# Local attention over eight units in one sequence, with key and query projections spread over its steps

## The chip, the cores and the metric

One core of a Trainium2 chip runs the whole program. The metric is the device time of one execution in microseconds (us), as the median of several runs. Beside it there is one profiled execution, from which all durations of single instructions come.

## The reference, cut to what matters

The input is a batch of 16 images of 64 x 64 pixels with 256 channels, in float32. Two layers follow each other, each with a group normalisation ahead of it and a residual addition behind it.

```python
# layer 0: linear attention over all pixels of an image (8 heads of 32)
x = x + _L0_conv_ref(_gn(x), L0_conv_w_qkv, L0_conv_w_out)
# layer 1: every pixel attends to the 7 x 7 pixels around it (8 heads of 32)
x = x + _L1_conv_ref(_gn(x), Wq, bq, Wk, bk, Wv, bv, emb0, emb1)

# inside layer 1
kp = _unfold(k, KSZ).reshape(B, H, W, HEADS, HS, K) + e.reshape(HEADS, HS, K)   # K = 49
scores = jnp.einsum('bhwnd,bhwndk->bhwnk', qh, kp)
attn = jax.nn.softmax(scores, axis=-1)
out = jnp.einsum('bhwndk,bhwnk->bhwnd', vp, attn)
```

The term `e` is a positional embedding: for the first four heads it depends on one axis of the 7 x 7 window, for the last four on the other.

## The kernel before, in words

**Layout.** An image lies in SBUF channel by channel: two tiles of 128 channels x 4096 pixels. Pixels are grouped into eight *strips* of 512 (`strip`, L463): a strip is a band of eight image columns over all 64 rows; strip 0 holds both edges. The order in which strips are treated is written out in `ORDER` and `KEYED` (top of the file). The instructions of TensorE, ScalarE, VectorE and SyncE stand in the order in which the program states them (`manual_schedule` with `ORDERED`); each engine works through its own list and waits on semaphores. All transfers are issued by SyncE, in that order too, at most eight of them in flight.

**One image** goes through these stages.

1. Layer 0 (`layer0`, L533 to L688): projections (L549), exponentials (L553), the context matmuls against the image's tokens (L567, the tokens come through `load_tokens`, L475), and the output products (L667), which add the residual to x.
2. Positional products and values. `positional_products` (L721) multiplies x with the positional weights; `positional` (L732) evacuates them from PSUM into the query tile `qq`, by `evacuate` (L710): ScalarE at L713, VectorE at L715. `store_rings` (L743) writes them to DRAM (`pos`); `load_rings` (L755) reads them back, shifted, into 16-partition strips of `qq` beside the query rows, together with a constant mask `io["ring"]` (L760, L761). The positional part of the scores thus becomes a part of the contraction. The values are projected strip by strip (`values_products`, L763, matmuls at L769), evacuated at L778 and written to a padded image `vpad` in DRAM (L783, L788). The PSUM for them comes from `banks()` (L392), which goes round four pairs of banks: the two tiles `double[0]` and `double[1]` of two banks each (called pd in the profile) and the four tiles `single` (ps) as two pairs.
3. For the first half of the heads (hg = 0) and then for the second (hg = 1): `keys_queries` (L792) projects all keys and then all queries of the half, two strips at a time (matmuls at L803), and evacuates them into `kaug` and `qq` (L713, L715). Then `local_attention` (L839) runs four *units*, in the order `UNITS`; a unit is a band of 16 image columns. The last pair of queries of a half is done behind the first step of its attention.

**A unit** is worked in nine *chunks* of eight key rows, two chunks to a step, the last alone: five steps. A step issues, on TensorE: the scores of its chunks (`scores`, L849, matmuls at L866, to one of the two pd tiles, then the exponential on ScalarE, L875 or L878, into a tile e), the weighted values of the step before (`weighted`, L912, L910; the sums of a unit stay in ps), and the softmax sums of the step before that (`summed`, L923, L940, into two banks). Between the two, VectorE adds the overlapping rows of neighbouring chunks (`both_chunks`, L891, L895), which the sums wait for. At a unit's end, ScalarE copies the weighted values out of PSUM (L1002), VectorE turns and inverts the sums (`finish`, L942: L947, L951, L952, L953), GpSimd multiplies (L966) and adds the residual (L974), and the finished strips are sent out (`store_out`, L1099, L1102).

**Values of a unit.** `load_window` (L827, L836) reads a unit's values from `vpad` into a window tile, four transfers for all nine chunks at once. There are two window tiles; the next unit but one is loaded when a unit has ended. The tokens of layer 0 use the same two tiles.

**The next image** is prepared meanwhile (`between0`, L1104, and `between1`, L1122): loading of its strips (L1113, L470), their statistics (L483), the group statistics with two small matmuls (`group_steps`, L268 and L277, in a part of a pd tile that `next_bank`, L403, names), the first two normalised strips (L303) and the first tokens.

At the start of each half, TensorE first fills the four pd banks with a large negative number (L983), since not every score position is written.

Of the kernel before, what the change touches and what calls it, by code (L numbers as in the profile page):

```python
# [10 lines left out]
F32 = mybir.dt.float32  # L11
# [8 lines left out]
P = 128  # L20
# [20 lines left out]
UNITS = (1, 2, 3, 0)  # L41
KEYED = (2, 3, 4, 5, 6, 7, 1, 0)
ORDER = (4, 5, 6, 7, 0, 1, 2, 3)
EDGE = (5, 3)

# [330 lines left out]
def attention_fast(tc, io, ok):  # L376
# [3 lines left out]
    with ExitStack() as ctx:  # L380
# [5 lines left out]
        turn = [0, 0]  # L386
# [5 lines left out]
        def banks():  # L392

            i = turn[1] % 4
            turn[1] += 1
            if i >= 2:
                return single[2 * i - 4 : 2 * i - 2], (0, 1)
            return [double[i][:, j] for j in range(2)], (i, i)

        def bank(name):  # L400
            return psum2()[:, 0]

        def next_bank(name):  # L403

            return double[(turn[0] + 1) % 2][:, 0, 64:]
# [43 lines left out]
        work = ctx.enter_context(tc.tile_pool(name="work", bufs=6))  # L449
        tail = ctx.enter_context(tc.tile_pool(name="tail", bufs=1))  # L450
        vwin = ctx.enter_context(tc.tile_pool(name="vwin", bufs=2))
# [4 lines left out]

        def window(name):
            return vwin.tile([P, 2 * NB * P], F32, tag="vw", name=name)
# [11 lines left out]
        def load_half(b, k):  # L470
            x = halves(b)[0][k]
            for s in ORDER:
                nc.sync.dma_start(x[:, strip(s)], xc[b, :, k, strip(s)])

        def load_tokens(b, q):  # L475

            t = window(f"xtok{b}_{q}")[:, : 8 * (C + 1)].rearrange("p (t c) -> p t c", c=C + 1)
            nc.gpsimd.memset(t[:, :, C : C + 1], 1.0)
            nc.sync.dma_start(t[:, :, :C], xt[b, q])
            return t  # L480
# [52 lines left out]
        def layer0(b, x, xn, mean, rstd, xtok, ready, midway=None):  # L533
# [30 lines left out]
            def context(p):  # L564
                for t in range(2):
                    for hg in range(2):
                        nc.tensor.matmul(  # L567
                            pc[hg][:, : C + 1],
                            eq[p][:, t, C + hg * P : C + (hg + 1) * P],
                            xtok[p // 4][:, 2 * (p % 4) + t],  # L570
                            start=(p == 0 and t == 0),
                            stop=(p == 15 and t == 1),
                        )
# [8 lines left out]
            for p in range(16 + 1):  # L582
# [6 lines left out]
                if 1 <= p <= 16:  # L589
                    context(p - 1)  # L590
                    if p % 4 == 0 and p // 4 + 1 < 4:
                        xtok[p // 4 + 1] = load_tokens(b, p // 4 + 1)
# [48 lines left out]
            w4 = window(f"w4_{b}")[:, : 8 * C].rearrange("p (h g c) -> p h g c", h=4, g=2)  # L641
# [113 lines left out]
        def load_rings(hg):  # L755
            for h in range(4):
                p0 = 64 * (h % 2) + 32
                row = pos[hg][0, RING, h]
                src = bass.AP(row.tensor, row.offset, [[4 * W, RING], [SLOTS * 4 * W, W], [1, W]])
                nc.sync.dma_start(qq[p0 + RING * hg : p0 + RING * hg + RING, h // 2], src)  # L760
                nc.sync.dma_start(qq[p0 + RING * (1 - hg) : p0 + RING * (1 - hg) + RING, h // 2], io["ring"])  # L761
# [30 lines left out]
        def keys_queries(b, hg, x):  # L792

            for what in range(2):
                for i in range(0, NS, 2):
                    if what and i == NS - 2:
                        yield
                    ps, engines = banks()
                    pair = KEYED[i : i + 2]
                    wgt = wq if what else wk  # L800
                    for a in range(2):
                        for k in range(2):
                            nc.tensor.matmul(  # L803
                                ps[a],
                                wgt[:, k, hg * P : (hg + 1) * P],
                                x[k][:, strip(pair[a])],
                                start=(k == 0),
                                stop=(k == 1),
                            )
                    for a in range(2):  # L810
                        for h in range(4):
                            rows = slice(h * HD, (h + 1) * HD)
                            d0 = 64 * (h % 2)
                            for u, p0, m, w, view in pieces(pair[a]):
                                src = view(ps[a][rows])
                                if what:
                                    dst = placed(qq[d0 : d0 + HD, h // 2], hg)[:, :, w : w + m]
                                else:
                                    dst = kaug[h // 2][d0 : d0 + HD, u, PAD : PAD + W, p0 : p0 + m]
                                dst = by_rows(dst, src)  # L820
                                if what and hg:

                                    order = "p r w -> p w r" if len(src.shape) == 3 else "p g r w -> p w g r"
                                    dst, src = dst.rearrange(order), src.rearrange(order)
                                evacuate(engines[a], dst, src, bias[rows, 2 * what + hg : 2 * what + hg + 1])

        def load_window(b, hg, t):  # L827


            vw = window(f"vw{b}_{hg}_{t}").rearrange("p (j c d) -> p j c d", j=2, d=P)  # L830
            v = vpad[b % 2]
            for j in range(2):
                for e, u in enumerate((2 * t + 2 * j, 2 * t + 1)):
                    row = v[u, 0, 0, hg * P : (hg + 1) * P]
                    src = bass.AP(row.tensor, row.offset, [[C, 64], [64 * C, NB], [1, P]])
                    nc.sync.dma_start(vw[64 * e : 64 * e + 64, j], src)  # L836
            return vw

        def local_attention(b, hg, x, y, vw, queries, after_scores, between, stored):  # L839
# [3 lines left out]
            outs, zs = single[:2], single[2:]  # L843
# [5 lines left out]
            def scores(t, c):  # L849
                ps = psum2()  # L850
                lo, hi = span(c)
                m = 16 * (hi - lo)
                for pl in range(2):
                    for e, u, w0, w1 in ((0, 2 * t, 0, 8), (1, 2 * t + 1, 2, 16), (0, 2 * t + 2, 10, 16)):
                        for ab in range(2):
                            rows = slice(64 * ab, 64 * ab + 64)
                            q = qq[rows, pl].rearrange("p (a c) -> p a c", c=W)
                            if hg == 0:
                                q = q[:, lo:hi, 16 * t + w0 : 16 * t + w1]
                                to = ps[64 * e : 64 * e + 64, ab, pl * m : (pl + 1) * m]  # L860
                                to = to.rearrange("p (r w) -> p r w", w=16)[:, :, w0:w1]
                            else:
                                q = q[:, 16 * t + w0 : 16 * t + w1, lo:hi]
# [9 lines left out]
                e = work_tile(f"e{b}_{hg}_{t}_{c}")[:, : 4 * m]  # L873
# [8 lines left out]
            def rows_of(c, e, r0, r1):  # L882
# [8 lines left out]
            def both_chunks(c, e, before):  # L891

                r0 = 8 * c - 2 * PAD
                part = rows_of(c, e, r0, 8 * c)
                nc.vector.tensor_tensor(part, part, rows_of(c - 1, before, r0, 8 * c), ALU.add)  # L895

            def products(to, j, h, c, e, r0, r1, stationary, **flags):
# [14 lines left out]
            def weighted(c, e, vw):  # L912
                if c == 0:

                    for i, to in enumerate(outs):
                        rows = slice(64 * i, 64 * i + 64)
                        nc.tensor.matmul(to, nb[rows], bits[rows, :1].to_broadcast([64, 512]), start=True, stop=False)
                for j in range(2):
                    for h in range(4):
                        v = vw[:, j, c, h * HD : (h + 1) * HD]  # L920
                        products(outs[j], j, h, c, e, *span(c), v, start=False, stop=(c == NB - 1))

            def summed(c, e):  # L923

                lo, hi = span(c)
                m = 16 * (hi - lo)
                r0, r1 = max(8 * c - 2 * PAD, 0), min(8 * c + 8 - 2 * PAD, W)
                for i in range(2):
                    a, z = max(r0, 32 * i), min(r1, 32 * i + 32)
                    for h in range(4 if a < z else 0):  # L930
                        pl, ab = divmod(h, 2)
                        pr = e[:, ab, pl * m : (pl + 1) * m]
                        dst = zs[i][h * HD : (h + 1) * HD]
                        if hg == 0:
                            pr = pr[:, 16 * (a - lo) : 16 * (z - lo)]
                            dst = dst[:, 16 * (a - 32 * i) : 16 * (z - 32 * i)]
                        else:
                            pr = pr.rearrange("p (w r) -> p w r", w=16)[:, :, a - lo : z - lo]
                            dst = dst.rearrange("p (w r) -> p w r", w=16)[:, :, a - 32 * i : z - 32 * i]
                        nc.tensor.matmul(dst, ones, pr, start=True, stop=True)  # L940

            def finish(i, t, r, pvs):  # L942

                for k in range(2):


                    nc.vector.transpose(r[:, k], zs[k])  # L947
                yield
                turned = r.rearrange("p k (a c) -> p (k a) c", c=HD)
                rc = small.tile([P, 2, 32], F32, tag="rc", name=f"rc{b}_{hg}_{t}")  # L950
# [579 lines left out]
```

## Time and profile before

| | |
|---|---|
| median of 3 runs | 5796.24 us (5793.12 to 5801.21) |
| the profiled execution | 5803.41 us, its span 5801.6 us |
| mean granted TensorE clock | 0.961 |
| TensorE matmuls busy | 5233.0 us of the span |
| VectorE, ScalarE, GpSimd busy | 3450.4, 2196.3, 1345.2 us |
| scores L866 | 27648 matmuls, 939.7 us busy |
| weighted values L910 | 18432 matmuls, 573.0 us busy |
| sums L940 | 10240 matmuls, 406.0 us busy, 150.1 us idle before them |
| key and query projections L803 | 2048 matmuls in four groups |
| overlap additions L895 | 1024, 758 ns each in the mean |
| evacuations L713 and L715 | 648 to 758 ns each for 32 x 512, in most groups |
| window loads L836 | 512 transfers of 288 KB |
| DMA | 540.81 MB, mean 93 GB/s |

How to read it: a group of instructions has the line of the kernel that issued it, its engine, its operation and its tiles; then its count, its busy time, the mean of one in ns, and the idle time of the engine just ahead of it with what ended that idle time ("releaser"). A float32 matmul of the program appears as two passes. A releaser "issue" means that the profile shows nothing that the engine waited for. The granted clock is a share of TensorE's full clock. In a table of stages the columns are: the stage in us, its length, the busy time of PE (TensorE matmuls), PEld (its weight loads), DVE (VectorE), ACT (ScalarE) and POOL (GpSimd), each with a count, then the clock, the mean busy share of the 16 DMA engines, and GB/s.

### The profile page before, as it was taken

What the parts mean: (1) busy time and instruction counts of PE and PEld (TensorE: products, weight loads), DVE (VectorE), ACT (ScalarE), POOL (GpSimd) and SP (SyncE); (2) the same over time, 40 slices, a digit from 0 to 9 for tenths busy, and PEclk for the clock granted to TensorE, in tenths of its full rate; (3) what the DMA queues carried; (4) which work ended last, traced back from release to release, by engine and by line L of the source; (5) the groups of instructions that cost most, each with busy time, mean ns of one, the idle gap of its engine ahead of it and who ended that gap; (6) DMA issues with size and microseconds to landing.
All of it is one profiled execution on the core that took longest, in us unless ns stands there. A gap on an engine that the chain in (4) does not pass through costs nothing.

```text
span 5801.6 us, 169268 instructions
## 1 busy us (share of the span) xinstructions
PE 5233.0 (90%) x75377; PEld 3593.3 (62%) x75377; DVE 3450.4 (59%) x5978; ACT 2196.3 (38%) x3089; POOL 1345.2 (23%) x1962
## 2 busy tenths in 40 slices
PE   7989899898998989989899898998989889898997
PEld 4656566565665666656666566665666566565665
DVE  4565656656566565665656556565575655756555
ACT  1341624426244261442514425153351533515335
POOL 3131131312313123130221302213032130321303
PEclk9999999999999999999999999999999999999999
DMA  4542725536164361644517345173450824517244
GB/s 122 108 104 50 138 58 112 108 58 131 50 121 99 62 132 45 126 94 78 120 41 132 97 78 119 34 136 93 78 120 32 149 80 90 116 31 142 80 78 88
DMA packets 751605, 540.81 MB, mean 93 GB/s; under 512 B 241408, under 2 KB 682368, under 8 KB 748416
## 3 DMA queue, kind: packets, MB, share of 16 engines
q1 hardware_dynamic: 750864, 529.89, 44.8%
q8 instruction: 592, 9.70, 0.7%
q14 instruction: 149, 1.22, 0.1%
HBM read 371.04 MB, written 158.73 MB: 91 GB/s over the span
## 4 chain that ended last, share of the span: by engine, by line
PE 75%; DVE 10%; issue 5%; ACT 5%; DMA 3%; SPq 1%; POOL 1%; DVEq 0%; ACTq 0%; POOLq 0%
PE pd L549 15%; PE pd L866 13%; PE ps L910 8%; PE pd L803 7%; PE ps L567 6%; PE ps L803 5%; PE ps L667 4%; PE pd L667 4%; ACT qq L713 4%; PE ps L940 4%; DVE e L895 3%; PE ps L769 3%; PE pd L769 3%; PE ps L724 2%; DVE qq L715 2%
## 5 line engine op out<-in xcount | busy, mean ns | idle before, releaser
L895 DVE TENSOR_TENSOR e<-e,e 128x384 f32<-128x384 f32 x1024 | 748.9, 758 | 765.7 <-PE ps L910 564.1
L866 PE MATMUL pd<-qq,kaug 64*64 64x112 f32 (+4 forms) x27648 | 939.7, 276 | 160.2 <-issue 65.0
L866 PEld LDWEIGHTS pd<-qq,kaug 64*64 64x64 f32 x27648 | 809.7, 138 | 322.3 <-issue 175.8
L549 PE MATMUL pd<-wqkv,img 128*128 128x512 f32 x2048 | 949.8, 609 | 3.2 <-DVE img L303 3.2
L553 ACT ACTIVATE eq<-pd 128x1024 f32<-128x1024 f32 x256 | 262.2, 1024 | 1077.8 <-PE pd L549 1077.8
L461 POOL TENSOR_TENSOR others<-others,rc 128x32 f32<-128x32 f32 x128 | 32.3, 252 | 2739.9 <-DVE rc L951 2739.7
L549 PEld LDWEIGHTS pd<-wqkv,img 128*128 128x128 f32 x2048 | 399.6, 196 | 412.6 <-issue 376.8
L556 DVE TENSOR_REDUCE qz<-eq 128x16 f32<-128x512 f32 x256 | 175.5, 686 | 768.4 <-ACT eq L553 768.4
L910 PE MATMUL ps<-e,vw 128*32 128x112 f32 (+1 forms) x18432 | 573.0, 260 | 62.7 <-issue 62.2
L878 ACT ACTIVATE e<-pd 128x896 f32<-128x896 f32 (+2 forms) x576 | 461.3, 835 | 423.1 <-PE pd L866 416.3
L875 ACT ACTIVATE e<-pd 128x896 f32<-128x896 f32 (+2 forms) x576 | 462.5, 838 | 404.0 <-PE pd L866 398.1
L713 ACT ACTIVATE qq<-ps,bias 32x512 f32<-32x512 f32 (+2 forms) x512 | 318.8, 648 | 740.7 <-DVE bias L708 665.5
L940 PE MATMUL ps<-e,ones 128*32 128x128 f32 (+2 forms) x10240 | 406.0, 266 | 150.1 <-DVE e L895 119.4
L910 PEld LDWEIGHTS ps<-e,vw 128*32 128x32 f32 x18432 | 416.7, 113 | 154.6 <-issue 118.5
L974 POOL TENSOR_TENSOR img<-img,r 128x320 f32<-128x320 f32 (+1 forms) x512 | 494.1, 995 | 0.0
L567 PE MATMUL ps<-xtok,eq 128*128 128x257 f32 x2048 | 483.4, 380 | 0.0
L567 PEld LDWEIGHTS ps<-xtok,eq 128*128 128x128 f32 x2048 | 387.3, 190 | 150.0 <-issue 107.1
L715 DVE TENSOR_SCALAR qq<-ps,bias 32x512 f32<-32x512 f32 (+2 forms) x416 | 311.8, 758 | 161.5 <-PE ps L803 155.5
L713 ACT ACTIVATE kaug<-pd,bias 32x512 f32<-32x512 f32 x256 | 173.9, 679 | 570.6 <-PE pd L803 567.7
L966 POOL TENSOR_TENSOR r<-r,r 128x512 f32<-128x512 f32 x256 | 342.2, 1358 | 139.8 <-DVE r L953 138.7
L940 PEld LDWEIGHTS ps<-e,ones 128*32 128x32 f32 x10240 | 253.5, 115 | 194.0 <-DVE e L895 157.4
L483 DVE BATCH_NORM_STATS2 st<-img 128x6 f32<-128x512 f32 x512 | 332.2, 680 | 9.1 <-DMA img<-in_xc 4.7
(142 smaller groups left out, 6613.3 us busy)
## 6 DMA issues: line engine op xcount, KB each, us to landing
vw<-vpad SPq DMA_DIRECT2D x512, 288.0 KB
img<-in_xc SPq DMA_DIRECT2D x256, 256.0 KB
xtok<-in_xt SPq DMA_DIRECT2D x64, 1024.0 KB
out<-img SPq DMA_DIRECT2D x256, 256.0 KB
vpad<-v SPq DMA_DIRECT2D x112, 512.0 KB
qq<-pos SPq DMA_DIRECT2D x128, 256.0 KB
qq<-in_ring SPq DMA_DIRECT2D x128, 256.0 KB
pos<-qq SPq DMA_DIRECT2D x128, 112.0 KB
```

What stands on the lines that cost most here:

```text
L549: nc.tensor.matmul(ps[:, t], xn[k][:, n0 : n0 + P], n.wqkv_sb[:, k, : 2 * C], start=(k == 0), stop=(k == 1))
L567: nc.tensor.matmul(pc[hg][:, : C + 1], eq[p][:, t, C + hg * P : C + (hg + 1) * P], xtok[p // 4][:, 2 * (p % 4) + t], start=(p == 0 and t = ...
L667: nc.tensor.matmul(py[a], w4[rows, h, hg, co * P : (co + 1) * P], qv[rows, 4 * hg + h, 8 * HD * i : 8 * HD * (i + 1)], start=(h == 0 and h ...
L713: nc.scalar.activation(dst, src, AF.Identity, bias=bias)
L803: nc.tensor.matmul(ps[a], wgt[:, k, hg * P : (hg + 1) * P], x[k][:, strip(pair[a])], start=(k == 0), stop=(k == 1),)
L866: nc.tensor.matmul(to, kaug[pl][rows, u, 8 * c : 8 * c + 8].rearrange("p r w -> p (r w)"), q, start=True, stop=True,)
L875: nc.scalar.activation(e.rearrange("p (a n) -> p a n", a=2), ps[:, :, : 2 * m], AF.Exp)
L878: nc.scalar.activation(e.rearrange("p (x r) -> p x r", r=hi - lo), src, AF.Exp)
L895: nc.vector.tensor_tensor(part, part, rows_of(c - 1, before, r0, 8 * c), ALU.add)
L910: nc.tensor.matmul(dst, stationary, pr, **flags)
L940: nc.tensor.matmul(dst, ones, pr, start=True, stop=True)
L974: nc.gpsimd.tensor_tensor(yv, xv, by_rows(add[:, :, a - w0 : e - w0], xv), ALU.add)
```

## The change

- The two halves' four units each become **one sequence** of eight (`SEQUENCE`), with 42 steps instead of twice 24. A blank of the pd banks is written ahead of the first two chunks of units 0 and 4.
- `keys_queries` is gone. A **job** projects the keys of one strip or the queries of half a unit (32 rows x 16 columns, `job_products`) into one bank, `single[3]`, and is evacuated in the next step (`place_job`), on ScalarE or VectorE (`job_engine`). 28 jobs stand in the steps 0 to 29 (`JOBS`); four (`AHEAD`) stand between the last value strips. A query job has six matmuls where a strip had two, since a unit is cut from three strips.
- The sums have **one bank** instead of two. They are written in three groups of rows (`SUMS`), each turned and inverted before the next is written (`reciprocals`); `LATE` says which chunks are summed in which step.
- The values are projected in the two pd tiles alone.
- Windows are loaded **by chunk pairs**: after a step's weighted values, that part of the window is filled for the unit two further on. The two window tiles are fixed tiles `vbuf`, with the chunk as the outer index; tokens are loaded in parts as well.
- The rings of the second half go to a quarter-size tile `qx` for its first unit and to quarters of `qq` for the others (`load_quarter`, in steps 19, 21 and 23).
- The work pool has 7 tiles instead of 6; the strip order is turned (6, 7, 0, 1, ...); the next image's first half of channels is loaded strip by strip from step 22, with its statistics in steps 27 to 34, group statistics in steps 35 to 37 in `single[3]`, and its first two normalised strips in steps 38 and 39. Outputs leave one strip per step (`send`).

```diff
-UNITS = (1, 2, 3, 0)
+SEQUENCE = ((0, 1), (0, 2), (0, 3), (0, 0), (1, 2), (1, 3), (1, 0), (1, 1))
 KEYED = (2, 3, 4, 5, 6, 7, 1, 0)
-ORDER = (4, 5, 6, 7, 0, 1, 2, 3)
+ORDER = (6, 7, 0, 1, 2, 3, 4, 5)
+LATE = ((0, 1), (2,), (3, 4, 5), (6, 7), (8,))
+SUMS = ((0, 18), (18, 42), (42, 64))
+AHEAD = (("k", 0, 2), ("k", 0, 3), ("k", 0, 4), ("q", 0, 1, 0))
+JOBS = {
+    0: ("q", 0, 1, 1),
+    1: ("k", 0, 5),
+    2: ("k", 0, 6),
+    3: ("q", 0, 2, 0),
+    5: ("q", 0, 2, 1),
...
+    29: ("q", 1, 1, 1),
+}
...
+        def load_rings():
+            for h in range(4):
+                dynamic_ring(0, qq, h, 0, W)
+                p0 = 64 * (h % 2) + 32 + RING
+                nc.sync.dma_start(qq[p0 : p0 + RING, h // 2], io["ring"])
+            for h in range(4):
+                dynamic_ring(1, qx, h, 32, 16)
...
+        def job_products(job, x, to):
+            what, hg = job[:2]
+            columns = slice(hg * P, (hg + 1) * P)
+            if what == "k":
+                for k in range(2):
+                    nc.tensor.matmul(to, wk[:, k, columns], x[k][:, strip(job[2])], start=(k == 0), stop=(k == 1))
+                return
...
+            def reciprocals(k, a, rc):
+                r0, r1 = SUMS[a]
+                n0, m = r0 // 2, (r1 - r0) // 2
+                to = turns[(3 * k + a) % 2][:, : HD * m]
+                nc.vector.transpose(to, sums_of(a))
+                z = to.rearrange("p (a c) -> p a c", c=HD)[:, :, 0]
+                nc.vector.reciprocal(rc[:, n0 : n0 + m], z)
+                watch(others, z, m)
...
             for step in range(len(groups) + 2):
                 new = None
+                if job:
+                    place_job(job, spare, job_engine(step - 1))
                 if step < len(groups):
                     k, g = groups[step]
                     new = (k, g, [(c, scores(k, c)) for c in range(2 * g, min(2 * g + 2, NB))])
+                    after_scores(step)
                 if held:
                     k, g, es = held
                     for c, e in es:
                         weighted(k, c, e)
+                    read(k, g)
...
                 if late:
                     k, g, es = late
                     kept += es
                     for c, e in kept:
                         if c in LATE[g]:
                             summed(k, c, e)
                     kept = [(c, e) for c, e in kept if c not in LATE[g]]
+                job = JOBS.get(step)
+                if job:
+                    job_products(job, x, spare)
                 if held:
                     for c, e in es:
                         if c:
                             both_chunks(SEQUENCE[k][0], c, e, before)
...
+        def job_engine(step):
+            return step % 5 not in (1, 4)
...
                 for i, s in enumerate(KEYED):
-                    pv = first[i] if i < 2 else banks()[0]
+                    pv = [double[i % 2][:, j] for j in range(2)]
...
+                    if i == 2:
+                        fold_bias(mean, wk, (0, 1), single[0])
+                        fold_bias(mean, wq, (2, 3), single[0])
                     if i == 3:
-                        load_rings(0)
+                        load_rings()
+                    if 3 <= i < 7:
+                        job = AHEAD[i - 3]
+                        job_products(job, x, single[i - 3])
+                        place_job(job, single[i - 3], 1)
+                    if i in (4, 5, 6, 7):
+                        load_window(b, i // 2 - 2, *((0, 4) if i % 2 == 0 else (4, NB)))
```

## The prediction

> **What bounds the kernel now.** I read, in order: busy time by engine, the stages of one image, TensorE's waits, then the PE and DMA timelines where these waits lie. The image is the one whose layer 0 starts at 2203.6 us and whose successor starts at 2561.0 us (357.4 us; all times below are us in it).
>
> ```profile
> PE 5233.0 (90%) x75377; PEld 3593.3 (62%) x75377; DVE 3450.4 (59%) x5978; ACT 2196.3 (38%) x3089; POOL 1345.2 (23%) x1962
> ```
>
> TensorE is the bound, but a tenth of the span it stands. Next, the stages (us, busy per engine, granted clock, DMA share, GB/s): value products; first-half projections; first-half attention; second-half projections; second-half attention.
>
> ```profile
> 2295.00:2363.19 68.19, 67.20 (x725) 55.26 (x721) 43.37 (x88) 7.61 (x9) 1.10 (x2) 1.00 0.30 58
> 2363.19:2390.49 27.30, 24.94 (x64) 10.75 (x61) 21.08 (x29) 17.88 (x29) 0.00 (x0) 1.00 1.03 162
> 2390.49:2460.71 70.22, 61.05 (x1778) 48.91 (x1776) 39.63 (x59) 38.71 (x56) 20.83 (x24) 0.90 0.62 134
> 2460.71:2493.98 33.27, 31.41 (x121) 14.56 (x117) 25.77 (x37) 21.15 (x34) 5.87 (x8) 0.95 0.95 117
> 2493.98:2561.02 67.04, 52.61 (x1725) 43.90 (x1724) 46.66 (x70) 34.32 (x50) 23.45 (x27) 0.96 0.42 110
> ```
>
> From 2363.19 on, TensorE idles 2.4 + 9.2 + 1.9 + 14.4 = 27.8 us, and the lowest clocks stand there. Who it waits for, over the whole run (us, times, longest):
>
> ```profile
> PE ps L940 <- DVE e L895: 119.4, 129, 3.0
> PE pd L983 <- ACT qq L713: 67.4, 32, 2.4
> PE pd L866 <- issue: 65.0, 56, 3.9
> PE ps L910 <- issue: 62.2, 50, 2.9
> PE pd L866 <- DVE gnm L270: 24.3, 15, 2.1
> ```
>
> Divided by 16 images: sums on the overlap additions 7.5; blanks on the query evacuation 4.2; "issue" 9.8 with L940's 29.6; scores on the next image's statistics 2.2 (with L279's 10.5); and the two first exponentials of each half (30.3 and 28.9) 3.7. Both starts are seen here:
>
> ```profile
> 2383.89 3.60 PE L803 MATMUL ps<-img,wqn 128*128 128x512 f32 x8
> ...
> 2390.17 0.39 PE L983 MATMUL pd<-bits,nb 32*128 32x512 bf16 x2 [2.36 <-ACT qq L713]
> 2390.49 1.36 PE L866 MATMUL pd<-qq,kaug 64*64 64x64 f32 x48
> ...
> 2401.64 2.56 PE L866 MATMUL pd<-qq,kaug 64*64 64x112 f32 x48 [1.91 <-ACT e L875]
> ...
> 2410.71 1.36 PE L866 MATMUL pd<-qq,kaug 64*64 64x64 f32 x48
> ...
> 2425.14 1.36 PE L866 MATMUL pd<-qq,kaug 64*64 64x64 f32 x48
> ```
>
> The last two are the first scores of successive units: 14.4 us, less 1.35 idle between them, is **13.0 us of TensorE work per unit** (2506.01 to 2521.80 less 2.9 gives the same). Last, the DMA under the values and projections, in stages: ring stores; value stores; ring loads; value stores; windows.
>
> ```profile
> 2344.00:2353.00 9.00, 8.77 (x41) 7.74 (x42) 7.38 (x15) 0.00 (x0) 0.00 (x0) 1.00 0.89 135
> 2353.00:2359.00 6.00, 6.00 (x29) 5.29 (x28) 2.64 (x4) 0.00 (x0) 0.00 (x0) 1.00 1.01 319
> 2359.00:2379.00 20.00, 19.74 (x82) 10.36 (x81) 13.46 (x21) 8.46 (x13) 0.00 (x0) 1.00 1.19 119
> 2379.00:2386.00 7.00, 7.00 (x17) 3.04 (x16) 5.37 (x9) 5.01 (x11) 0.00 (x0) 1.00 0.89 289
> 2386.00:2403.00 17.00, 12.73 (x176) 7.26 (x178) 7.29 (x10) 13.59 (x23) 0.00 (x0) 0.87 1.05 210
> ```
>
> DMA is full for nearly 60 us. Today the 27 us of projections hide this; it is the cover that the change takes away.
>
> **What the Trainium skill says.** "SBUF — State Buffer", section "Door 1: The DMA port swizzle": 16 partitions reach 4 of 16 ports, measured there 104 GB/s. The ring loads write 16 partitions each; the trace has 119 GB/s for them against 319 for the value stores: it agrees. The same page, "Who interferes with whom": a VectorE operation with two SBUF inputs contends with GpSimd reads. It agrees: one overlap addition takes 0.56 us alone, 1.43 (2437.0 on) while GpSimd ends a unit. "TensorE: Matmul & The Clock Gate", "What's actually happening": idle TensorE falls to half clock, and needs some 3.4 us of work to return. It agrees: after the 2.85 us wait that ends at 2558.2 the next image's first matmul shows 1222 ns where its median is 592. Its "LDWEIGHTS" section: a weight load takes columns / 1.2 ns, 107 ns for 128; no row here shows it bare.
>
> **The change, part by part.** One image, from the first ring loads on.
>
> *Start of attention.* The eight first-half ring transfers are issued where they were (after the fourth value strip), behind the same stores, so they should land when they do now, **2379**. TensorE gets there as follows. It has value strips one and two done at 2340.3; the third now reuses the first pair of banks, freed only after VectorE's positional evacuations (to 2343.9 in the new pairing: 8 x 0.92 from 2336.5) and two value evacuations (1.25): at 2345.2, a new wait of 4.9. Six strips of 3.5, bias folds of 1.8 and half clock (1.5) for the first give 2345.2 + 24.3 = 2369.5; four jobs ahead, 4 x 1.76 (16 projection passes take 7.03, a job is 4 of them), give 2376.5. So it waits 2.5 us more for the rings, and the first wait costs nothing of its own: it lies under the rings. First scores at 2379 instead of 2390.5, with 4 of 32 jobs done instead of nearly 32.
>
> *Work from there.* 8 units x 13.0 = 104.0. Key jobs 13 x 1.76 = 22.9. Query jobs 15: six short matmuls of 160, 256 and 96 columns in place of two of 512, written to PSUM in short runs. Floor 1.75 (same columns), ceiling 2.4 (every short pass held to the 196 ns that a weight load shows); the scores, also written in short runs, reach 0.9 columns per ns against 1.2 of the projections; I take 2.0, so 30.0. Blanks 4 x 0.39 = 1.6. Sums: 36 matmuls per unit, not 40, in one bank: -1.0 in all. Together 157.5, to 2536.5.
>
> *Evacuations* move into the steps. A step with a job is 3.1 scores + 1.6 weighted + 1.0 sums + 1.8 job = 7.5 on TensorE; ScalarE has 4 x 0.7 + 2 x 0.84 = 4.5, VectorE, for the ten jobs that it places, 4 x 0.75 + 2 x (0.56 to 1.43) + statistics 0.65 + a third of the reciprocals 0.6 = up to 7.1. Behind the evacuation in ScalarE's queue stand that step's exponentials, for which TensorE asks 4.7 us into the next step; behind VectorE's stand the additions, asked for one step later. Both have 3 us to spare; TensorE hides them. Without that cover each job step would grow by up to 3 us.
>
> *Waits.* The second half's start vanishes (1.9 + 1.8, and its share of half clock), as do the first half's (2.4 + 1.9), one drain (0.6) and the statistics wait, since its bank is no longer a score bank (2.4). What stays: additions and one drain 3.5 of 7.4 (GpSimd's tail now starts a step earlier, so less of it falls on the drain); "issue" 6 of 10.1, because most of these stalls lie in or just after the 1.15 MB window bursts (2418, 2432, 2451, 2513), which become five of at most 256 KB; bounds 3 and 12. New small waits 1 (scores of a unit's first chunk on queries placed a step before). Half clock 4 of 7.8. Sum 14.5 of 35.6; bounds 8.5 and 29.
>
> *Queues.* SyncE issues 20 window transfers per unit instead of 4, each waiting for the weighted matmuls of its chunk pair; output stores that wait for GpSimd (7 us) stand before them. The windows are wanted ten steps later, so nothing is late. The second half's rings follow in quarters, six steps ahead.
>
> *Sum.* 2536.5 + 14.5 = 2551.0 against 2561.0: -10. I round to **-9 us per image**, the rings being 1 us uncertain. 16 x 9 = 144: 5803.4 (span 5801.6, and 1.8 around it) - 144 = 5659 for a profiled execution; this one is 7 above the median of the runs (5796.2), so 5652, say **5650**.
>
> **The rivals.**
> *Fetch and additions are cured* (stalls 8.5): -16 per image, 5803 - 256 - 7 = 5540. For it: steps are longer by a job, and bursts small. Against: "issue" stalls are not proven to come from bursts; the initial backlog now meets dense matmuls.
> *Part of the cover is missed*: rings or query jobs cost 4 to 8 us more (query jobs at 2.4 alone are 6): 5710 to 5790.
> *Slower: the DMA backlog takes the projections' place.* The first weighted matmuls, about 2388, need the first window, queued behind rings, 0.25 MB of the second half's rings (2.2 us) and a value store (1.5); at 195 GB/s its half lands near 2386. If instead the window comes only when all of today's backlog is through (2402), TensorE stands 14 us with 28 jobs still ahead: +5 per image, 5796 + 80 = 5876. It decides from a first weighted matmul later than 2397. For it: the DMA is saturated, SyncE holds eight transfers in flight. Against: the first window is issued ahead of the last three value stores.
> That the change does not do what it says I exclude: the built order has the jobs between the steps.
>
> **How the numbers follow.** Forecast 0.55 (5600 to 5700); cured 0.13; part missed 0.12 (0.03 of it within 0.2%, what a measurement of this kernel can tell from no change); backlog 0.20 (0.02 within). Faster 0.77, same 0.05, slower 0.18. The range from 5520 to 5790 leaves out the backlog and little of the cured case.
>
> **What would show it.** No projection stage; first scores some 11 us earlier after the value products, waiting for ring transfers about 2.5 us; value products waiting 4 to 5 us for a value evacuation; no wait on L270 by scores; "issue" under 110 us in all; query jobs at 1.75 to 2.4 us. Wrong if scores wait for rings over 6 us, if weighted matmuls wait for the window, or if job steps exceed 8 us.

## The result, and the profile after

The changed kernel takes **5892.39 us** in the median (5889.42 to 5896.39, 4 runs) against 5798.73 us before (5793.12 to 5804.82, 4 runs beside them): a ratio of **1.0162**, 95% interval 1.0144 to 1.0179. It is slower by 1.6%; the forecast was 5650 us. The profiled execution's span is 5887.6 us, its clock 0.971 (before 0.961).

First the image that the prediction worked in, in two stages: values and jobs ahead, from the first value products after the bias; attention. The columns are the stretch, its length, busy time (and count) of PE, PEld, DVE, ACT and POOL, the granted clock, the DMA share and GB/s. Before:

```profile
2335.96:2390.49 54.53, 51.68 (x210) 33.57 (x208) 40.29 (x61) 24.44 (x36) 0.00 (x0) 1.00 0.88 153
2390.49:2561.02 170.53, 145.07 (x3618) 107.37 (x3616) 112.07 (x164) 94.18 (x140) 50.15 (x59) 0.93 0.61 121
```

After:

```profile
2370.88:2416.20 45.32, 36.22 (x189) 28.53 (x188) 19.14 (x31) 17.49 (x24) 0.00 (x0) 0.96 0.89 126
2416.20:2599.83 183.63, 160.33 (x3701) 123.75 (x3701) 109.28 (x185) 115.56 (x168) 54.50 (x95) 0.99 0.45 131
```

The first stage became 9.2 us shorter, where 11.5 was forecast; attention became 13.1 us longer. One image is not the mean: over the 14 inner images of each trace, by the starts of the matmuls, layer 0 and its outputs are 0.6 us longer (3.2 in this image), positional products to first scores 9.7 shorter (67.01 to 57.35), attention 15.0 longer (171.4 to 186.4), together +5.9. In the kernel after, attention so taken begins with the scores' wait for the rings; if that wait is put to the stage before it, as the prediction did, the stage is 7.0 shorter (67.0 to 60.0).

Whom TensorE waits for in the kernel after (us over the run, times, longest):

```profile
PE ps L1014 <- DVE turn L1020: 98.8, 61, 4.0
PE ps L854 <- DVE kaug L737: 79.9, 64, 1.4
PE pd L808 <- DVE v L817: 77.9, 16, 4.9
PE ps L854 <- ACT kaug L735: 35.9, 64, 1.0
PE pd L935 <- DMA qq<-in_ring: 34.7, 15, 3.1
...
PE pd L935 <- issue: 2.5, 2, 2.0
```

L854 and L836 are the products of query and key jobs, L735 and L737 the evacuations on ScalarE and VectorE. All waits of jobs for an evacuation, ten such lines, sum to **221 us, 13.8 per image**; before, there is no such wait. The stalls without a shown wait ("issue") fell from 157 us to 5, and all of TensorE's waits other than the jobs' from 554 to 373. So the change removed what it was expected to remove, 181 us, and paid more for one new wait; its matmuls are also busy 35 us longer (5268 against 5233). One job step of the kernel after shows it, first TensorE, then VectorE:

```profile
2469.18 1.98 PE L836 MATMUL ps<-img,w 128*128 128x512 f32 x4
2471.10 1.56 PE L935 MATMUL pd<-qq,kaug 64*64 64x112 f32 x48
2472.59 0.97 PE L979 MATMUL ps<-e,vbuf 128*32 128x112 f32 x32
2473.38 0.47 PE L1014 MATMUL ps<-e,ones 128*32 128x32 f32 x16
2475.15 2.09 PE L854 MATMUL ps<-img,wqn 128*128 128x160 f32 x12 [1.30 <-DVE kaug L737]
```

```profile
2470.34 1.25 DVE L1027 STREAM_TRANSPOSE r<-rc 128x1024 f32<-128x1024 f32 x1
2471.51 0.65 DVE L504 BATCH_NORM_STATS2 st<-img 128x6 f32<-128x512 f32 x1
2472.09 3.01 DVE L737 TENSOR_SCALAR kaug<-ps,bias 32x512 f32<-32x512 f32 x4
```

The key job's bank is full at 2471.2. VectorE starts to empty it at 2472.09, behind a transposition and a statistic, and needs 3.01 us for the four heads. The next job, to the same bank, could have started at 2473.85 (its wait is 1.30) and starts at 2475.15.

### The profile page after: what moved, and what is told of

It reads as the page before. It is cut to its first block, busy times and chain, and to the rows that moved or that the text cites. A ratio compares the mean times of both kernels' runs of the same rounds, so it can differ in the third digit from the quotient of the medians.

```text
span 5887.6 us, 177452 instructions
## 1 busy us (share of the span) xinstructions
PE 5268.3 (89%) x76401; PEld 3816.2 (65%) x76401; DVE 3075.9 (52%) x5818; ACT 2424.1 (41%) x3377; POOL 1418.3 (24%) x2690
## 3 DMA queue, kind: packets, MB, share of 16 engines
q14 instruction: 191, 1.56, 0.1%
## 5 line engine op out<-in xcount | busy, mean ns | idle before, releaser
L735 ACT ACTIVATE qq<-ps,bias 32x512 f32<-32x512 f32 (+1 forms) x864 | 599.9, 700 | 959.2 <-DVE bias L730 662.5
L935 PE MATMUL pd<-qq,kaug 64*64 64x112 f32 (+5 forms) x24192 | 787.0, 269 | 48.0 <-DMA qq<-in_ring 34.7
L854 PE MATMUL ps<-img,wqn 128*128 128x160 f32 (+2 forms) x3072 | 550.3, 329 | 140.7 <-DVE kaug L737 79.9
L854 PEld LDWEIGHTS ps<-img,wqn 128*128 128x128 f32 x3072 | 481.7, 194 | 230.4 <-DVE kaug L737 97.1
L735 ACT ACTIVATE kaug<-ps,bias 32x512 f32<-32x512 f32 (+1 forms) x704 | 414.0, 609 | 520.1 <-PE ps L836 514.6
L808 PE MATMUL pd<-wvn,img 128*128 128x256 f32 x2048 | 530.1, 416 | 81.9 <-DVE v L817 77.9
L836 PE MATMUL ps<-img,w 128*128 128x512 f32 x1024 | 502.8, 613 | 88.5 <-DVE kaug L737 25.6
L808 PEld LDWEIGHTS pd<-wvn,img 128*128 128x128 f32 x2048 | 423.6, 210 | 176.1 <-DVE v L817 84.3
L979 PE MATMUL ps<-e,vbuf 128*32 128x112 f32 (+1 forms) x18432 | 527.7, 252 | 0.7 <-issue 0.7
L588 PE MATMUL ps<-vbuf,eq 128*128 128x257 f32 x2048 | 483.6, 380 | 0.0
L1014 PE MATMUL ps<-e,ones 128*32 128x128 f32 (+1 forms) x9216 | 352.4, 265 | 111.4 <-DVE turn L1020 98.8
```

Source lines behind the costliest of these rows:

```text
L588: nc.tensor.matmul(pc[hg][:, : C + 1], eq[p][:, t, C + hg * P : C + (hg + 1) * P], tokens_of(p // 4)[:, 2 * (p % 4) + t], start=(p == 0 an ...
L735: nc.scalar.activation(dst, src, AF.Identity, bias=bias)
L808: nc.tensor.matmul(pi[:, t], x[k][:, n0 : n0 + P], wv[:, k], start=(k == 0 and t == 0), stop=(k == 1 and t == 1))
L836: nc.tensor.matmul(to, wk[:, k, columns], x[k][:, strip(job[2])], start=(k == 0), stop=(k == 1))
L854: nc.tensor.matmul(dst, wq[:, k, columns], src, start=(k == 0 and i == 0), stop=(k == 1 and i == len(parts) - 1),)
L935: nc.tensor.matmul(to, kaug[pl][rows, u, 8 * c : 8 * c + 8].rearrange("p r w -> p (r w)"), q, start=True, stop=True,)
```

## The experiments

**My theory after the result**: the one job bank is the bound. Products, four evacuations in a row and the next products take turns on it, 2.0 + 2.8 to 3.0 us and what stands ahead of the evacuation in its engine's queue, while the rest of a step is only 2.7 us. **Rivals**: another limit ends last anyway (additions, the sums bank), so that the wait only has a name; VectorE is overloaded; the smaller window transfers do harm or do nothing. Ratios are to the kernel before, run beside each on the same chip. It took 5784 to 5799 us there, so the medians of two rows can differ by up to 15 us for that reason alone; the ratios are free of it.

| run | what is altered, in the kernel after unless said | median us | ratio (95%) |
|---|---|---|---|
| after | | 5892.39 | 1.0162 (1.0144 to 1.0179) |
| e1_split | two heads on each engine | 5959.55 | 1.0307 (1.0289 to 1.0324) |
| e2_act | jobs on ScalarE alone | 5842.86 | 1.0101 (1.0084 to 1.0118) |
| e3_whole | whole windows | 5912.98 | 1.0221 (1.0204 to 1.0238) |
| e4_before_pairs | before, with chunk-pair windows | 5827.83 | 1.0080 (1.0063 to 1.0097) |
| e5_staged | bank emptied by one operation | 5715.71 | 0.9857 (0.9825 to 0.9889) |
| e6_norm | normalisations a step later | 5859.10 | 1.0101 (1.0069 to 1.0134) |
| e7_banks | four pairs of value banks | 5872.71 | 1.0125 (1.0092 to 1.0157) |
| e8_all | e5 to e7, earlier strip loads | 5586.57 | 0.9641 (0.9616 to 0.9666) |
| e9_all_recip | e8, reciprocals first | 5598.11 | 0.9663 (0.9640 to 0.9686) |
| e10_staged_whole | e5, whole windows | 5683.53 | 0.9818 (0.9793 to 0.9843) |
| e11_all_whole | e8, whole windows | 5592.32 | 0.9672 (0.9654 to 0.9691) |
| e12_staged_reload | e5, earlier strip loads | 5641.05 | 0.9748 (0.9731 to 0.9764) |

### Which engine empties the bank

```diff
-                    place_job(job, spare, job_engine(step - 1))
+                    place_job(job, spare, None)     # e1_split: evacuate(h % 2, ...) for head h
+                    place_job(job, spare, 1)        # e2_act
```

> Every job inside a step is evacuated by both engines, two heads each. Theory (the one job bank is the bound: its products wait 221 us in all, because four evacuations of 0.69 to 0.75 us in a row do not fit between two jobs): an evacuation takes 1.4 us instead of 2.8 to 3.0, the waits of the products (0.95 behind ScalarE, 1.3 behind VectorE) nearly vanish, under 40 us in all, and the time is 5892 - 190 = 5700 (5660 to 5740). Rival (another limit ends last in a step, such as the additions or the sums bank, and the wait only changes its name): the sums' waits grow by as much as the products' shrink, and the time stays above 5850.

> Every job is evacuated by ScalarE alone, none by VectorE; the number of evacuations on one engine in a row stays four. Theory (what counts is the length of the row of four, whichever engine does it): a row takes 2.76 instead of 3.0, so the products' waits stay, at 0.6 to 1.0 each, 150 to 220 us in all, and the time is 5860 (5830 to 5900). Rival (VectorE, with additions and reciprocals before the evacuation in its queue, is what is late): the 125 us of waits on VectorE's evacuations vanish, and the time is 5770.

**e1_split was a miss**, and the trace says why. The evacuation of one job, VectorE and then ScalarE:

```profile
2526.24 0.74 DVE L737 TENSOR_SCALAR qx<-ps,bias 32x512 f32<-32x512 f32 x1 [0.23 <-PE ps L854]
2527.73 0.74 DVE L737 TENSOR_SCALAR qx<-ps,bias 32x512 f32<-32x512 f32 x1 [0.75 <-ACT qx L735]
```

```profile
2527.02 0.68 ACT L735 ACTIVATE qx<-ps,bias 32x512 f32<-32x512 f32 x1 [1.28 <-DVE qx L737]
2528.51 0.68 ACT L735 ACTIVATE qx<-ps,bias 32x512 f32<-32x512 f32 x1 [0.81 <-DVE qx L737]
```

The two engines take turns: each copy waits for the other engine's. So the four copies last from 2526.24 to 2529.19, 2.95 us, as long as on one engine, and now every job holds up both queues: the scores wait 27 us for exponentials that stand behind it. This tested nothing of the theory's first half, but it agrees with it: the row is no shorter, and the waits did not shrink (267 us). The Trainium skill ("PSUM — Partial Sum Buffer", "PSUM bank collisions raise a hardware error") says that two engines may use different groups of 32 partitions of one bank at once, and that guarding by bank is the simple version. The heads are such groups, so by that page the turns need not be taken; that they come from a guard by whole bank fits the trace, but no run here tried the finer one.

**e2_act** came within what the theory said: the row is shorter (0.68 instead of 0.75 each, and nothing of VectorE's ahead of it), the waits fall from 221 to 156 us, but do not go. That VectorE alone was the trouble is excluded by that; its queue was a part of it, as the kernel is 0.6% faster.

### The bank is freed at once

```diff
+            if engine is None:      # to: a 512-pixel strip of SBUF that is free in this step
+                column = 2 * (what == "q") + hg
+                nc.scalar.activation(to, ps, AF.Identity, bias=bias[:, column : column + 1])
+                ps = to
...
-                evacuate(engine, dst, src, column)
+                moved(h, dst, src)  # heads 1, 3: nc.scalar.copy; heads 0, 2: nc.vector.tensor_copy
```

> A job's bank is emptied by one ScalarE operation of 128 x 512, bias added, into a strip of SBUF that is free in that step; from there ScalarE and VectorE move two heads each, with no bank between them. Theory (the time for which the one job bank is held, four evacuations in a row, sets a job step): it is held 0.6 us after the products instead of 2.8 to 3.0, the products' waits fall from 221 us to under 30, and the time is 5892 - 190 = 5700 (5650 to 5750), although ScalarE and VectorE together do more work. Rival (the additions, the sums bank or ScalarE's exponentials end last as soon as the bank does not): the sums' or the scores' waits take over and the time stays above 5840.

This is the test that e1 was meant to be. One job in e5_staged, on ScalarE and VectorE:

```profile
2462.46 0.69 ACT L872 ACTIVATE img<-ps,bias 128x512 f32<-128x512 f32 x1
2463.18 2.13 ACT L864 COPY qq<-img 32x512 f32<-32x512 f32 x2
```

```profile
2463.18 1.19 DVE L866 COPY qq<-img 32x512 f32<-32x512 f32 x2 [2.91 <-ACT img L872]
```

The bank is read for 0.69 us. From SBUF both engines move heads to the same tile at the same time, so in e1_split it was not the tile written that made them take turns. Both engines are busier than in the kernel after (ScalarE 2596 us against 2424, VectorE 3179 against 3076, together 5775 against 5500), and the kernel is 3% faster: 5715.71. The same kind of step, on TensorE:

```profile
2464.75 2.09 PE L854 MATMUL ps<-img,wqn 128*128 128x160 f32 x12
...
2469.06 0.47 PE L1030 MATMUL ps<-e,ones 128*32 128x32 f32 x16
2469.45 1.98 PE L836 MATMUL ps<-img,w 128*128 128x512 f32 x4
```

The step takes 4.70 us (2464.75 to 2469.45) instead of 5.97, and no job waits any more: all ten lines are gone from the waits. **The job bank's holding time was the cause of these waits**: it was cut, while both engines got more to do. A part went into another wait, as the rival has it: the sums' wait for the turned sums grew from 98.8 to 156.2 us. At one place of each image, first VectorE, then TensorE of e5_staged:

```profile
2497.58 0.69 DVE L504 BATCH_NORM_STATS2 st<-img 128x6 f32<-128x512 f32 x1 [5.82 <-DMA img<-in_xc]
```

```profile
2499.65 1.51 PE L1030 MATMUL ps<-e,ones 128*32 128x128 f32 x24 [6.00 <-DVE turn L1036]
```

The strip whose statistics VectorE wants is late: in SyncE's own queue eight window transfers stand ahead of its load,

```profile
2486.72 6.62 SPq L913 DMA_DIRECT2D vbuf<-vpad  x8
2493.38 1.06 SPq L1239 DMA_DIRECT2D img<-in_xc  x2
```

and the steps have become short enough for it to be waited for.

```diff
+                    if step == 30 and more:         # in after_scores, ahead of the window transfers
+                        for s in (2, 3, 4):
+                            nc.sync.dma_start(x_next[0][:, strip(s)], xc[b + 1, :, 0, strip(s)])
```

> The staged evacuation and the earlier strip loads with their statistics one step later, alone: no later normalisation, no further value banks. Theory (the 6.0 us at the sums come from the late strips alone): 5716 less 15 x 6 = 5626 (5610 to 5650). Rival (the sums' waits come from VectorE's queue in general): above 5680.

As the theory has it: 5641, and the sums' wait is 91.7 us, VectorE's wait for strips 74 instead of 145. The three strips' statistics stand one step later, too, and how much of the gain is due to that was not tried alone.

### The window transfers

```diff
                     if k < 6:
-                        load_window(b, k + 2, 2 * g, min(2 * g + 2, NB))
+                        if g == 4:
+                            load_window(b, k + 2, 0, NB)
```

> The windows are loaded as before the change: four whole transfers when a unit's last chunk pair has been used, instead of four per chunk pair. Theory (the stalls for which the profile shows no wait, 157 us before and 5 after, come from the 1.15 MB bursts): they return, 100 to 160 us in all, part of it in place of waits for the job bank, and the time is 5970 (5930 to 6040). Rival (they went away with the new order of the steps, not with the pieces): they stay under 20 us and the time stays within 10 us of 5892.

> The kernel before with one part of the change alone: two fixed window buffers, laid out by chunk, loaded by chunk pairs as they come free. Theory (as for the run with whole windows): the 157 us of stalls without a shown wait fall under 20; additions and reciprocals take back a part, so the time is 5680 (5640 to 5740). Rival: the stalls stay, and the time is 5797 within 10.

> The staged evacuation with the windows loaded whole. With the waits for the job bank gone, nothing covers TensorE's stalls without a shown wait. Theory (bursts of 1.15 MB cause them, and in the run with whole windows the job bank's waits covered most): they come back, 60 to 130 us in all, and the time is 5790 (5750 to 5840). Rival (the new order of steps, not the pieces, removed them): within 20 of 5716.

> The version with everything together (5587), its windows loaded whole. With the strip loads already ahead of the windows, smaller pieces have nothing left to cost. Theory (pieces spare TensorE the stalls without a shown wait): these rise from 11 to 60 or more, and the time is 5587 + 55 = 5640 (5615 to 5670). Rival (20 transfers per unit in SyncE's queue cost as much as they save): 5570 to 5600.

The stalls without a shown wait do depend on the pieces: whole windows give 38 us of them instead of 5 (e3_whole), 58 instead of 3 (e10), 36 instead of 11 (e11), and chunk pairs in the kernel before 48 instead of 157. But **my theory's time came out in none of the four**, and in three of them the rival's did not either, because the pieces cost elsewhere. In the kernel before with chunk pairs:

```profile
PE ps L938 <- DVE e L893: 144.5, 161, 3.0
...
PE pd L864 <- DMA qq<-in_ring: 51.6, 21, 4.4
```

109 us of stalls are gone. Against that, scores wait 52 us for the second half's rings, which SyncE now issues behind window transfers, in one image at 2477.7, in the kernel before at 2458.3:

```profile
2462.39 14.14 SPq L835 DMA_DIRECT2D vbuf<-vpad  x20
...
2477.73 0.40 SPq L759 DMA_DIRECT2D qq<-pos  x1
```

The additions take 25 more, ScalarE's copies 16, the group statistics 11, and matmuls at a lower clock (0.954 against 0.961) are busy 26 us longer: +21 in all, of the 25 by which its span grew. In e10 the stalls come back, +55, but the sums' wait falls by 89 as the strips are in time (VectorE waits 7 us for them instead of 145). With the strips seen to (e11 against e8), +25 of stalls stand against -25 of the sums' wait: 5592 and 5587, ratios whose intervals overlap. This is e11's rival: no gain of loading by chunk pairs is left once the strips are in time. On the way there whole windows cost 20 us (e3: stalls +33, matmuls busy +19, sums' wait -19). In e10 they saved 32 by the medians, but the intervals of its ratio and of e5's overlap, so that saving is not sure.

### The start and the end of an image

```diff
-                    if 38 <= step < 40:
-                        normalise(xn_next, x_next, *gn, ORDER[step - 38])
+                    if 39 <= step < 41:             # e6_norm
+                        normalise(xn_next, x_next, *gn, ORDER[step - 39])
...
+                    pv = single[2 * i - 4 : 2 * i - 2] if i in (2, 3) else [double[i % 2][:, j] for j in range(2)]
```

In e7_banks the bias products move behind the fourth strip as well, to another bank.

> The next image's first two normalisations stand one step later in VectorE's queue (steps 39 and 40). They wait there for GpSimd's rstd, which is queued behind a unit's end, and the last reciprocals stand behind them, for which TensorE waits 4.0 us at each image's end. Theory: 3 of the 4.0 us go, 16 x 3 = 48: 5845 (5830 to 5860). Rival (the next image's first products then wait for the normalisations, or the drain waits for its last additions instead): within 10 of 5892.

> The third and fourth value strip get the four other banks once the positional products are evacuated, as before the change. The prediction: the 4.9 us wait lies under the ring loads, so only the scores' wait for the rings grows: within 25 of 5892, less the half clock after that wait (3.3 us in 10 of 16 images, if it isn't taken over by the wait for the rings). Rival (the ring loads are issued behind the fourth strip's store, so they come earlier by what the strips gain): 16 x 4.9 to 16 x 8 less, 5765 to 5815.

e6_norm: 33 us less, two thirds of what was expected. The longest wait at the image's end falls from 3.96 to 2.0; then the last additions, slow beside GpSimd (2.39 us for two), hold the transposition up. The cause in the kernel after, GpSimd and then VectorE:

```profile
2594.54 0.71 POOL L316 TENSOR_TENSOR gnr<-gnv,neghalf 128x2 f32<-128x2 f32 x1
```

```profile
2595.28 1.00 DVE L338 TENSOR_SCALAR img<-img,gnm,gnr 128x512 f32<-128x512 f32 x2 [2.31 <-POOL vbuf L500]
...
2597.14 0.57 DVE L1020 STREAM_TRANSPOSE turn<-ps 128x384 f32<-128x384 f32 x1
```

GpSimd's rstd (0.71 us of work) came at the end of a unit's 7.7 us, and VectorE's reciprocals stood behind what waits for it. The profile names L500, a fill that GpSimd does just before; the operand that VectorE waits for is gnr.

e7_banks: the value strips' 77.9 us of waits are gone, and the scores' wait for the rings rises by 55, from 34.7:

```profile
PE pd L935 <- DMA qq<-in_ring: 90.0, 29, 4.9
```

The bias products' waits rise by 12.5 (13.8 to 26.3). In all, TensorE waits 13 us less and its matmuls are busy 9 us less, which half clock after the 4.9 us wait would explain. Its interval overlaps that of the kernel after in the table, so the gain is not sure; that most of the wait lay under the rings is. A part of the rival is true, too: the first ring load is issued 32.3 us after an image's first positional products instead of 36.7, and the scores' last wait for rings ends at 57.9 instead of 60.1 (means of the inner images).

### Together

> The staged evacuation with the later normalisations, the four value banks, and one thing more: with the job bank free, VectorE stands 5.8 us per image at the statistics of a strip whose load is issued behind eight window transfers (6.6 us of SyncE's queue), and the last sums stand behind it, 6.0 us. Here these three loads are issued ahead of that step's window transfers, and the statistics that read them stand one step later. Theory (each is a wait of its own): 5716 less 33 and 20 as measured alone, less 15 x 6 = 90: 5573 (5540 to 5620). Rival (the sums' waits take over again): above 5650.

> As the run before, with the sums' transposition and reciprocal ahead of the overlap additions in VectorE's queue in every step. Theory (the sums bank, read by VectorE only after up to 2.4 us of additions, is the next single bank to be waited for): 10 to 30 less than the run before. Rival (the additions, now later, hold up the next sums): same or up to 20 more.

e8_all takes 5586.57 us, 3.6% under the kernel before (0.9616 to 0.9666), in the middle of what was expected: the gains add up, as they do when each wait has a place of its own. From e5's ratio, 0.9857, the gains of e12 (0.0109), e6 (0.0061) and e7 (0.0037) lead to 0.9650; 0.9641 was measured. TensorE's longest waits are now the scores' for the rings, 90 us, and the sums' for turned sums, 64. Moving the reciprocals ahead (e9) only changed the name: the sums' wait for turned sums goes, that for additions rises from 21 to 74 us. That theory fell.

## Why the prediction was wrong, step by step

**The step that failed is "Evacuations move into the steps"**, with its sentence "Both have 3 us to spare; TensorE hides them." Two things are wrong in it.

1. *The step is too long.* I took 3.1 + 1.6 + 1.0 + 1.8 = 7.5 us. The rows of 48 scores (1.56) and 32 weighted matmuls (0.97) already hold both chunks; I doubled them, and the sums' (0.47) with them. A job step without a wait takes 4.7 (e5_staged). Even the sum as it stands leaves 3.0 us to ScalarE (7.5 less 4.5), but 0.4 to VectorE (7.5 less 7.1). The sign "if job steps exceed 8 us" was set by the same length: the step shown above takes 5.97 and is too long. The prediction's own 13.0 us per unit, 2.6 per step, would have told me: 2.6 + 1.8 is 4.4, not 7.5.
2. *The cover was counted per engine, and the bank was not counted.* Even at the right length both engines have room (they are busy 2424 and 3076 us of 5888). What has none is the bank: 2.0 us of products and 2.8 to 3.0 of evacuation, in turn, want 4.8 to 5.0 of a step of 4.7, and each thing that stands ahead of the evacuation comes on top. The price that I did write, "without that cover each job step would grow by up to 3 us", names the right place. It was not among the rivals.

In the sum the jobs' wait for their bank was put at nothing: "new small waits 1" stands there for the scores' wait on queries, which came to 0.5 (8.0 / 16), and the jobs' to 13.8. The difference between -10 and +5.9 per image, term by term:

| term | predicted | measured | difference |
|---|---|---|---|
| new small waits, with the jobs' for their bank | 1 | 0.5 + 13.8 | +13.3 |
| additions, sums, drain | 3.5 | 6.9 | +3.4 |
| key jobs, 13 | 1.76 each | 1.92 each | +2.1 |
| stage up to the end of the wait for the rings | -11.5 | -7.0 | +4.5 |
| stalls without a shown wait | 6 | 0.3 | -5.7 |
| layer 0 | 0 | +0.6 | +0.6 |

These sum to +18.2, 2.3 more than the 15.9. That rest is not assigned: half clock within attention, taken at 4, was not measured by itself, and the prediction's image is 1.4 us shorter than the mean of the 14 (357.4, 358.8).

What held:
- *Start.* Value products waiting 4.9 us for a value evacuation (4.87 in 16 images), scores waiting 2.5 for the rings (34.7 / 15 = 2.3), the first of these waits mostly under the rings (e7). Half clock after it was taken at 1.5 and costs some 3.2 in 11 of 16 images: 6.63 and 5.41 us for strips that take 5.16 and 3.72 in the others (granted clock 0.64 from 551.1 to 563.0, 0.86 from 2380.2 to 2391.0).
- *Query jobs* at 2.0 (2.02 from start to start), and *no wait of scores on the next image's statistics*.
- *Stalls without a shown wait* under 110, but the reason given, the bursts, is only part of it: with the change's order of steps and whole bursts there are 38 (e3), or 58 without the job bank's waits (e10), not 157.

What also failed: *"they should land when they do now"* of the first ring loads. They stand behind the fourth value strip's store, and so behind the new 4.9 us wait: the first is issued 36.7 us after the image's first positional products instead of 32.4 (34.5 in an image whose value strips run at full clock, 37.7 in one where they do not), and the scores' wait for them ends at 60.1 instead of the 55.4 that 2379 stands for. This is the +4.5 of the table. And "nothing is late" of SyncE's queue. The windows are not late; what stands behind them is, in e4 the rings, in e5 the strips. *The slower rival*, the DMA backlog, did not happen: the first weighted matmuls stand at 2423.16, 7.0 us after the rings, without a wait for their window. The time ended on its side through another mechanism. With the bank freed and the strips' loads ahead (e12), the ratio is 0.9748, just what the forecast asks of this kernel (5650 / 5796 = 0.975). That is luck in part: the terms above miss in both directions.

## What to carry to other kernels

When work is spread into the steps of another loop, count the cover for every resource that it takes in turn, and first for the single buffer, here one PSUM bank: producer time + queue ahead of the consumer + consumer time against the step's length, taken from start to start of the same row in successive steps. If it does not fit, shorten the holding, not the work: one full-width copy out of PSUM and cheaper moves from SBUF were more work and 3% less time. And a queue that issues many small transfers delays what is issued behind them; look there before calling a moved transfer free.

## What the runs showed that I had not expected

- A ScalarE copy of 128 x 512 out of PSUM takes 0.69 us, as long as one of 32 x 512 (0.68): four heads at once cost as much as one. From SBUF, key heads of 32 x 512 take 0.42 us on VectorE in the median (0.75 out of PSUM) and 0.62 on ScalarE.
- A window transfer takes 0.64 to 0.83 us of SyncE's queue, with whatever it waits for there (2.55 for four, 6.62 for eight, in e5_staged), so 20 per unit are 13 to 17 us, as long as a unit's own work on TensorE (13.0) or longer.
